# Bias network of a deformable attention: the last addition by transfers, the third layer on four pairs of keys at a time

## Chip, core and metric

One NeuronCore of a Trainium2 chip runs the whole program in one launch. The metric is the device time in microseconds (us), float32 throughout. Engines are named as the profile names them: PE (TensorE, matrix products), PEld (its weight loads), DVE (VectorE), ACT (ScalarE), POOL (GpSimd) and SP (SyncE, which here only issues transfers).

## What is computed

The program is a chain of four blocks on a tensor of 2 x 512 x 32 x 32. The change lies in the first block, an attention with 8 heads whose 64 keys per (image, head) are sampled at learned positions. Every score gets a bias from a small network on the distance of query and key, evaluated for each of 8 x 2 x 1024 x 64 pairs:

```
pos  = grid_q[:, :, None, :] - grid_kv[:, None, :, :]
bias = sign(pos) * log1p(abs(pos))
bias = relu(bias @ cpb_w1 + cpb_b1)        # 2 -> 128
bias = relu(bias @ cpb_w2 + cpb_b2)        # 128 -> 128
bias = (bias @ cpb_w3 + cpb_b3)            # 128 -> 1
sim  = einsum('bhid,bhjd->bhij', qh, kh) + bias
attn = softmax(sim, axis=-1)
out  = einsum('bhij,bhjd->bhid', attn, vh)
x    = x + out_w @ out + out_b             # then a two-layer perceptron with gelu
```

Blocks 2 to 4 (another attention, a non-local block, a gated block) are not touched.

## The kernel before

**Stages.** A prologue normalises the input, projects queries (`query`), transposes the input (`flip_x`) and computes the first keys' positions (`Chain`). The main stage, a loop at line 910 over 256 pairs `p` of keys, evaluates the bias network and, between its pieces, everything else of the attention. Then come the projection `po` (L1014), the perceptron (L1079) and the other blocks.

**A key** here is one key of two heads, that is 2 x 1024 pairs; 8 groups `g` (4 pairs of heads, 2 images) of 64 keys make 512. The step number `n` in the text counts keys.

**First layer.** `first(n)` (L374, DVE) adds a row and a column feature and clips at zero, 128 hidden units by 1024 queries, once for each head, from a table `tab`. Tables come from DRAM (`tab_load`, L152, SP) for `TK` = 16 keys at a time and are scaled on ACT (`tab_scale`, L164). There are four buffers `h1`, so DVE runs at most two keys ahead.

**Second layer.** `second(p, o)` (L610, PE) multiplies by a quarter `o` of the 128 outputs, 32 columns at a time, so that four products, one for each 512 queries, lie side by side on the 128 partitions of `ph` (two buffers). ACT clips them and adds the bias into `r{o}` (L619). The quarters are arranged so that the third layer's weights could be taken into the second layer's: what is left of a weight is its sign. `combine` (L625, DVE) adds quarter 1 to 0 and quarter 3 to 2 with the relative sign `rel`. `join(p)` (L628, POOL) is a transfer that adds `r2` to `r0` in memory. In `r0` there are then 32 sums per query, on 32 partitions for each of four blocks of queries, for two keys `i`.

**Third layer.** `third(g, u)` (L651, PE) sums these with a column of signs `cw3` into `psims`, four keys a time, four products of 32 columns side by side. The scores' own product (`scores`, L636) is accumulated into the same bank.

**Attention.** `attend` takes a finished group: `evict` (ACT), `flip` (PE), `top`, `sub`, `total`, `norm` (DVE) and `exp` (ACT), `back` (PE), `keep_` (ACT). `prepare` makes the next group's keys and values, and `chain` the positions of later groups; its 36 taps (L221, DVE) run beside the network.

**Order.** Every instruction of this stage is pinned to the order in which the program issues it on its engine. `at(n, when, fn)` puts `fn` behind the second layer's product of step `n` (`when` 0 or 1: half a step), and the loop at line 910 runs it:

```
for p in range(NK // 2):
    for o in range(4):
        n = 2 * p + o // 2
        second(p, o)
        if o == 1 and p:
            combine(p - 1, 2)
            join(p - 1)
        elif o == 3:
            combine(p, 0)
        elif n + 2 < NK and o % 2 == 0:
            first(n + 2)
        run(n, o % 2)
```

A queue of transfers (SP's, POOL's) also works in this order: an issue that waits holds up what is behind it.

**Weights.** In the prologue `order` sorts the four quarters of each of 32 rows by the sign of the third layer's weight, so that the signs of 0 and 1, and of 2 and 3, are mostly equal for a row, with some 30 small operations on POOL.

Of the kernel before, what the change touches and what calls it, by code (L numbers as in the profile page):

```python
# [16 lines left out]
P = 128  # L17
# [4 lines left out]
TK = 16  # L22
# [14 lines left out]
    ("L0_conv_cpb_w1", 2), ("L0_conv_cpb_b1", 1), ("L0_conv_cpb_b2", 4), ("L0_conv_cpb_w3", 4),  # L37
# [18 lines left out]
_CONSTS = [("ident", P), ("grid", 2 * J), ("gridf", J), ("npx", 1), ("npy", 8), ("sel3", 2)]  # L56
_CAT, _n = {}, 0
# [3 lines left out]
NCONST = _n  # L61


@with_exitstack
def conv_seq(
# [5 lines left out]
    consts: bass.AP,  # L71
    qkv_w: bass.AP,
# [53 lines left out]
    with ExitStack() as ctx_l0:  # L126
# [21 lines left out]
        def tab_load(ch, j0=0):  # L148

            g, c0 = divmod(ch * TK, J)  # L150
            tab = tabp.tile([P, TK, 2, 2, 32], F32, name="tab")
            nc.sync.dma_start(  # L152
                tab[:, j0:].rearrange("p i h a q -> p (i h a q)"),
                fd[g, c0 + j0 : c0 + TK, :]
                .rearrange("j f -> (j f)")
                .unsqueeze(0)
                .to_broadcast([P, (TK - j0) * P]),
            )
            return tab
# [13 lines left out]
        cpbw = l0.tile([P, 2 * P], F32, name="cpbw")  # L173
# [18 lines left out]
        class Chain:  # L192
# [126 lines left out]
            def put(self, i, b):  # L319

                nc.sync.dma_start(
                    fd[(self.k0 + i) * B + b].rearrange("(i m) f -> m i f", m=4),
                    self.lg[b * J : (b + 1) * J, i * P : (i + 1) * P],
                )
# [7 lines left out]
        cw3 = l0.tile([P, 39], F32, name="cw3")  # L332
        rel = l0.tile([P, 2], F32, name="rel")

        def order(to, of, w3, pool):

            n = w3.shape[2]
            gp = nc.gpsimd
            m = pool(9 * n).rearrange("p (i n) -> p i n", n=n)
            g, same, swap, other, keep_ = (m[:, 0:4], m[:, 4], m[:, 5], m[:, 6], m[:, 7])  # L340
            tmp, nswap = m[:, 8], m[:, 0]
            pin(nc.vector.tensor_scalar(g, w3, 0.0, None, ALU.is_ge))
            for d, k in ((same, 2), (swap, 1)):
                gp.tensor_tensor(d, g[:, 0], g[:, k], ALU.subtract)
                gp.tensor_tensor(d, d, d, ALU.mult)
            gp.tensor_tensor(tmp, swap, same, ALU.mult)
            gp.tensor_tensor(swap, same, tmp, ALU.subtract)
            gp.tensor_scalar(same, same, -1.0, 1.0, ALU.mult, ALU.add)
            gp.tensor_tensor(keep_, swap, same, ALU.add)
            gp.tensor_scalar(other, keep_, -1.0, 1.0, ALU.mult, ALU.add)  # L350
            gp.tensor_scalar(nswap, swap, -1.0, 1.0, ALU.mult, ALU.add)

            def mix(i, *parts):
                t = pool(of.shape[2])
                for j, (k, mask) in enumerate(parts):
                    d = to[:, i] if j == 0 else t
                    gp.tensor_tensor(d, of[:, k], mask.to_broadcast([P, of.shape[2]]) if n == 1 else mask, ALU.mult)
                    if j:
                        gp.tensor_tensor(to[:, i], to[:, i], t, ALU.add)

            mix(0, (0, keep_), (1, other))
            mix(1, (1, same), (2, swap), (0, other))
            mix(2, (2, nswap), (1, swap))
            gp.tensor_copy(to[:, 3], of[:, 3])
# [22 lines left out]
        with tc.tile_pool(name="a", bufs=1) as a, tc.tile_pool(name="aps", bufs=3, space=PSUM) as aps, tc.tile_pool(  # L387
# [9 lines left out]
            qw = a.tile([P, KC, P], F32, name="qw")  # L397
            nc.scalar.dma_start(qw, qkv_w[:, 0])
# [4 lines left out]
            for k in range(1, KC):  # L403
                nc.sync.dma_start(xn[k].rearrange("p (b n) -> p b n", b=B), x_dram[k])
                if k == 1:
                    nc.sync.dma_start(offw, off_w)
                    nc.sync.dma_start(cpbw, cpb_w)
            nc.sync.dma_start(kvw, qkv_w[:, 1:3])
# [55 lines left out]
            room, used = h1p.tile([P, 2, 32, 32], F32, name="h1").rearrange("p h y x -> p (h y x)"), [0]  # L464

            def part(n):
                used.append(used[-1] + n)
                return room[:, used[-2] : used[-1]]

            wb = part(8).rearrange("p (s i) -> p s i", s=4)  # L470
            w3 = v("L0_conv_cpb_w3").unsqueeze(2)
            pin(nc.vector.tensor_scalar(wb[:, :, 0:1], w3, 0.0, 2.0, ALU.is_ge, ALU.mult))
            pin(nc.vector.tensor_scalar(wb[:, :, 0:1], wb[:, :, 0:1], -1.0, None, ALU.add))
            nc.gpsimd.tensor_tensor(wb[:, :, 1:2], w3, wb[:, :, 0:1], ALU.mult)
            nc.gpsimd.tensor_tensor(wb[:, :, 1:2], wb[:, :, 1:2], v("L0_conv_cpb_b2").unsqueeze(2), ALU.mult)
            order(sb3, wb, w3, part)
            for i in range(2):
                nc.gpsimd.tensor_tensor(rel[:, i : i + 1], sb3[:, 2 * i, 0:1], sb3[:, 2 * i + 1, 0:1], ALU.mult)
            nc.gpsimd.memset(cw3, 0.0)
            for t in range(4):  # L480
                ts_ = slice(32 * t, 32 * t + 32)
                nc.gpsimd.tensor_copy(cw3[ts_, 7 + 8 * t : 8 + 8 * t], sb3[ts_, 0, 0:1])
            w2r = part(P)
            w3r = cpbw[:, P : 2 * P]
            pin(nc.scalar.activation(w2r, w3r, AF.Abs))
            nc.gpsimd.tensor_tensor(w2r, w2r, cpbw[:, 0:P], ALU.mult)
            order(w2a, w2r.rearrange("p (s o) -> p s o", s=4), w3r.rearrange("p (s o) -> p s o", s=4), part)
# [32 lines left out]
            query(2, 0)  # L520
            ch.offsets()
# [13 lines left out]
            ch.feature()  # L535

            tab0 = tabs[0] = tabp.tile([P, TK, 2, 2, 32], F32, name="tab")
            for u0 in range(0, 8, 4):
                pfb = apk.tile([P, 4, 2, 2, 32], F32, name=f"pfb{u0}")
                for u in range(4):  # L540
                    key = 16 * u + u0 // 4
# [13 lines left out]
            for b in range(B):  # L555
                ch.put(0, b)
                if b == 0:
                    nc.sync.dma_start(
                        tab0[:, 8:].rearrange("p i h a q -> p (i h a q)"),
                        fd[0, 8:TK, :].rearrange("j f -> (j f)").unsqueeze(0).to_broadcast([P, 8 * P]),  # L560
                    )
            tabs[1] = tab_load(1)
            ch.spread(1)
            ch.coordinate(1)
            first(0)
            queried(2, 1, 2)
# [3 lines left out]
            flip_x(1, 3, act)  # L570
            queried(2, 3)
# [5 lines left out]
            for k in range(2, KC):  # L577
                for t in range(NT // 512):
                    flip_x(k, t, dve)
                    flipped(k, t)  # L580
                if k == 2:
                    first(1)

# [4 lines left out]
        with tc.tile_pool(name="hid", bufs=3) as hid, tc.tile_pool(name="sm", bufs=1) as sm, tc.tile_pool(name="hps", bufs=2, space=PSUM) as hps, tc.tile_pool(  # L588
# [40 lines left out]

            def scores(g):  # L630
# [15 lines left out]
            def third(g, u):  # L646
                kb, i = divmod(u, 8)
                p = (g * J + 4 * u) // 2
                for m in range(4):
# [3 lines left out]
                            lhsT=cw3[:, 7 - i : 39 - i],  # L653
                            rhs=rs[p + m // 2, 0][:, m % 2, :],
                            start=False,
                            stop=(i == 7),
# [3 lines left out]
                for i in range(2):  # L660
                    del rs[p + i, 0]

            def prepare(g):
# [53 lines left out]
                def keys():  # L717

                    for half in range(2):
                        for h in range(2):  # L720
                            hs = slice(h * DH, (h + 1) * DH)
                            to = kblk[hs, g % 2, :, half, :].rearrange("p k (m s i) -> p s k m i", m=4, s=4)
                            pin(
                                nc.scalar.activation(
                                    to[:, 2 * half + h],
                                    st["pk"][hs, 0, :].rearrange("p (m k i) -> p k m i", m=4, k=2),
                                    AF.Identity,
                                    scale=DH**-0.5,
                                )
                            )  # L730

                def values():
                    for h in range(2):
# [3 lines left out]
                                vblk[hs, g % 2, h, :].rearrange("p (k m i) -> p k m i", k=2, m=4),  # L737
                                st["pk"][hs, 1, :].rearrange("p (m k i) -> p k m i", m=4, k=2),
# [36 lines left out]
            def attend(g, n, step):  # L775
# [4 lines left out]
                def evict(kb):  # L780
                    if kb == 0:
                        st["simt"] = sm.tile([P, 2, 512], F32, name="simt")
# [16 lines left out]
                def top(kb):  # L799
                    if kb == 0:  # L800
                        st["mx"] = sm.tile([P, 2, 16], F32, name="mx")
                        st["e"] = sm.tile([P, 16, J], F32, name="e")
# [24 lines left out]

                def norm(i):
                    den, is_ = st["den"], slice(8 * i, 8 * i + 8)
                    if i == 0:  # L830
                        pin(nc.vector.reciprocal(den, den))
                    e = st["e"][:, is_]
                    pin(nc.vector.tensor_tensor(e, e, den[:, is_].unsqueeze(2).to_broadcast([P, 8, J]), ALU.mult))
# [12 lines left out]
                def keep_(s):  # L846
# [6 lines left out]
                    (10, 0, exp, 0), (11, 0, exp, 1), (12, 0, exp, 2), (13, 0, exp, 3),  # L853
                    (14, 1, total, 0), (16, 1, total, 1), (18, 1, norm, 0), (20, 1, norm, 1),
                    (22, 1, back, 0), (22, 1, back, 1), (23, 0, keep_, 0), (23, 1, keep_, 1),
# [10 lines left out]
            for i in range(4):  # L866
                ax, j = i % 2, 8 + 4 * (i // 2)
# [838 lines left out]
```

## Time and profile before

| what | value |
|---|---|
| median of three runs | 2807.63 us (2806.73 to 2810.03) |
| the profiled execution | 2807.81 us, of which the span is 2806.0 us |
| prologue, 0 to 47 us | PE busy 34.39 us |
| bias network, 47 to 2002 us | PE busy 1951.08, DVE 1867.33, ACT 1324.89, POOL 219.55 us of 1955 |
| `po`, 2002 to 2051 us | PE busy 48.14 us |
| rest, 2051 to 2806 us | PE busy 724.05 us |

In a group's row of the profile, `out<-in xcount | busy, mean ns | idle before, releaser`, the idle time is that of the engine just before these instructions. A float32 product is recorded as two MATMULs. A transfer's time to landing counts from its issue to its semaphore.

### The profile page before, as it was taken

The page shows a single profiled execution, that of the slowest core. Times are in us where ns is not written, and L with a number is a line of the kernel's source. Part 1 is how long each engine was busy: PE and PEld are TensorE (multiplying, and loading weights), DVE is VectorE, ACT ScalarE, POOL GpSimd, SP SyncE. Part 2 cuts the span into 40 slices and gives each one's busy share as a digit, 9 for nine tenths or more (in the row PEclk, how much of TensorE's full clock was granted, in tenths as well). Part 3 has the DMA queues.
Part 4 walks back from the last instruction along what each step waited for, and adds up shares of the span by engine and source line. Part 5 has one row for each costly group of instructions (what it writes and reads, how often), then busy time and mean ns, then how long its engine had stood idle before and what let it go on. Part 6 is the DMA issues. An engine that isn't in the chain of part 4 may idle for free.

```text
span 2806.0 us, 47481 instructions
## 1 busy us (share of the span) xinstructions
PE 2757.7 (98%) x20280; PEld 1002.8 (36%) x20280; DVE 2275.4 (81%) x2473; ACT 1514.6 (54%) x1790; POOL 233.9 (8%) x318
## 2 busy tenths in 40 slices
PE   8999999999999999999999999999999999999996
PEld 4333333333333323333332333333344444455543
DVE  6999999999999999999999999999754554523545
ACT  6676676767667666766666676666311101001244
POOL 2111111111111111111111111111000000000000
PEclk9999999999999999999999999999999999999998
DMA  3444444434344443434453345443300000000001
GB/s 128 83 88 84 91 92 85 89 79 88 83 92 92 84 85 83 91 84 85 97 121 84 84 85 117 97 88 73 79 29 23 15 23 23 37 39 0 1 1 60
DMA packets 58835, 200.57 MB, mean 71 GB/s; under 512 B 5600, under 2 KB 14944, under 8 KB 53888
## 3 DMA queue, kind: packets, MB, share of 16 engines
q0 software_dynamic: 36864, 134.23, 25.5%
q1 hardware_dynamic: 21328, 62.79, 5.8%
q8 instruction: 159, 2.61, 0.4%
q10 hardware_dynamic: 432, 0.52, 0.1%
q14 instruction: 52, 0.43, 0.0%
HBM read 58.84 MB, written 4.46 MB: 23 GB/s over the span
## 4 chain that ended last, share of the span: by engine, by line
PE 53%; issue 37%; POOL 5%; DVE 2%; ACT 2%; DMA 0%; POOLq 0%; ACTq 0%; DVEq 0%
PE ph L610 24%; POOL r L628 5%; PE A L1079 4%; PE C L1079 4%; PE D L1079 4%; PE pr L1326 2%; PE B L1079 2%; PE po L1014 2%; PE psim L651 2%; PE pg L1222 1%; PE pz L1428 1%; PE pa L1317 1%; PE pu L1256 1%; PE pscore L1399 1%; PE pr L1439 1%
## 5 line engine op out<-in xcount | busy, mean ns | idle before, releaser
L610 PE MATMUL ph<-h,w2a 128*32 128x512 f32 x16384 | 1794.4, 593 | 2.2 <-ACT r L619 1.3
L619 ACT ACTIVATE r<-ph,sb 128x1024 f32<-128x1024 f32 x1024 | 1142.7, 1116 | 635.7 <-PE ph L610 617.9
L374 DVE CUSTOM_DVE_ANT_1 h<-tab 128x1024 f32<-128x1024 f32 x1024 | 1208.1, 1224 | 36.0 <-PE ph L610 35.4
L610 PEld LDWEIGHTS ph<-h,w2a 128*32 128x32 f32 x16384 | 533.4, 109 | 1213.6 <-issue 858.0
L625 DVE SCALAR_TENSOR_TENSOR r<-r,rel,r 128x1024 f32<-128x1024 f32 x512 | 657.7, 1285 | 32.7 <-ACT r L619 32.1
L628 POOL DMA_DIRECT2D r<-r x256 | 220.4, 861 | 1764.8 <-DVE r L625 1673.8
L164 ACT ACTIVATE tab<-tab,vec 128x256 f32<-128x256 f32 x252 | 137.3, 545 | 0.0
L651 PE MATMUL psim<-r,cw 128*32 128x512 f32 x1024 | 135.7, 593 | 0.8 <-DMA r<-r 0.8
L1119 ACT COPY u<-A 128x512 f32<-128x512 f32 x16 | 9.4, 586 | 146.9 <-PE A L1079 146.9
L1098 ACT ACTIVATE h<-h,vec 128x512 f32<-128x512 f32 x32 | 23.1, 721 | 113.3 <-DVE h L1101 113.3
L1101 DVE TENSOR_TENSOR h<-C,u 128x512 f32<-128x512 f32 x32 | 22.1, 691 | 48.1 <-PE C L1079 47.8
L1079 PE MATMUL A<-xn,w 128*128 128x512 f32 x128 | 60.2, 593 | 0.8 <-DVE x L1021 0.8
L651 PEld LDWEIGHTS psim<-r,cw 128*32 128x32 f32 x1024 | 33.9, 110 | 74.7 <-issue 73.7
L1079 PE MATMUL C<-hT,w 128*128 128x512 f32 x128 | 60.3, 592 | 0.0
L1079 PE MATMUL A<-h,w 128*128 128x512 f32 x128 | 60.1, 592 | 0.0
L1014 PE MATMUL po<-q,vwo 128*128 128x512 f32 x128 | 55.8, 594 | 0.0
L1326 PE MATMUL pr<-x,A 128*128 128x512 f32 x128 | 55.1, 592 | 0.0
L221 DVE SCALAR_TENSOR_TENSOR acc<-q,vec,acc 128x128 f32<-128x128 f32 (+3 forms) x88 | 46.9, 533 | 0.8
L1139 DVE TENSOR_TENSOR x<-D,x 128x512 f32<-128x512 f32 x32 | 22.1, 691 | 25.9 <-PE D L1079 25.9
L1139 DVE TENSOR_TENSOR x<-C,x 128x512 f32<-128x512 f32 x32 | 22.1, 690 | 24.8 <-PE C L1079 24.8
L1267 POOL MEMSET M<- 128x512 f32 x2 | 1.0, 524 | 443.9 <-DVE ss L1203 443.9
L1222 PE MATMUL pg<-xt 128*128 128x512 f32 (+3 forms) x128 | 36.4, 439 | 0.8 <-ACT xt L1220 0.6
(287 smaller groups left out, 1730.8 us busy)
## 6 DMA issues: line engine op xcount, KB each, us to landing
r<-r POOLq DMA_DIRECT2D x256, 512.0 KB, 4.5
tab<-fd SPq DMA_DIRECT2D x31, 1024.0 KB, 5.8
lw<-in_l_w_dram SPq DMA_DIRECT2D x5, 1024.0 KB
x<-in_x_dram SPq DMA_DIRECT2D x4, 1024.0 KB, 6.7
w<-in_mlp_w_dram SPq DMA_DIRECT2D x8, 512.0 KB, 3.7
w<-in_mlp_w_dram SPq DMA_DIRECT2D x16, 256.0 KB, 3.1
out_dram<-r SPq DMA_DIRECT2D x8, 512.0 KB, 2.7
xn<-in_x_dram SPq DMA_DIRECT2D x3, 1024.0 KB
```

The lines of the kernel that those rows point to most:

```text
L164: return nc.scalar.activation(tf, tf if src is None else src[:, :, :, ax, :], AF.Identity, bias=0.0 if ax == 0 else v("L0_conv_cpb_b1"), s ...
L221: pin(nc.vector.scalar_tensor_tensor(dst, src, wt_, dst, ALU.mult, ALU.add))
L374: nc.vector._custom_dve(TENSOR_ADD_SAT, out=h1[:, h], in0=tab[:, j, h, 0, :].unsqueeze(1).to_broadcast([P, 32, 32]), in1=tab[:, j, h, 1, : ...
L610: nc.tensor.matmul(ph[t * 32 : (t + 1) * 32, i, :], lhsT=w2a[:, o], rhs=h1s[2 * p + i][:, h, half * 512 : (half + 1) * 512], start=True, s ...
L619: pin(nc.scalar.activation(r, ph, AF.Relu, bias=sb3[:, o, 1:2]))
L625: pin(nc.vector.scalar_tensor_tensor(r0, r1, rel[:, i : i + 1], r0, ALU.mult, ALU.add))
L628: nc.gpsimd.dma_start(rs[p, 0], rs.pop((p, 2)), accum_op=ALU.add)
L651: nc.tensor.matmul(psims[g, kb][m * 32 : (m + 1) * 32, :], lhsT=cw3[:, 7 - i : 39 - i], rhs=rs[p + m // 2, 0][:, m % 2, :], start=False, s ...
L1014: nc.tensor.matmul(po, lhsT=vwo[:, k * B + t // 2, o * P : (o + 1) * P], rhs=q[:, k, ts_], start=(k == 0), stop=(k == KC - 1),)
L1079: nc.tensor.matmul(banks[bank], lhsT=a[an][k], rhs=b_[bn_][k], start=(i < 4 and k == 0), stop=(k == n - 1), skip_group_check=True,)
L1222: nc.tensor.matmul(pgs[i], lhsT=xt[:, i * P : (i + 1) * P], rhs=xt[:, i * P :], start=(t == 0), stop=(t == 7),)
L1326: nc.tensor.matmul(pr, lhsT=A[b][:, k, o * P : (o + 1) * P], rhs=x[:, k, ns], start=(k == 0), stop=(k == KC - 1),)
```

## The change

**The outputs that are left are added further.** After `join`, `r0` holds for each block of queries 32 sums for key 0 and 32 for key 1. The change adds neighbouring rows too: for key 0 the sums on odd partitions to the even ones, for key 1 the even to the odd. `shift(p)` is two SP transfers that copy the rows in question into a new tile `xs` (six buffers), one row aside; `fold(p)` is two POOL transfers that add the other rows of `r0`. Then `xs` holds 16 sums of each of the two keys, interleaved, on the 32 partitions. So a product of the third layer covers two keys, and four pairs of keys go into one set of four products.

**Positions.** `shift(p)` stands at step 2p + 4, `fold(p)` at 2p + 5, `third(g, u)` at 64g + 8u + 14 (before: at 64g + 4u + 6). Scores move from 64g + 6 to 64g + 10, the attention of a group by three steps, and its back part by six more.

**Signs.** All eight outputs that are added (four quarters of an even and an odd row) must stand so that each addition joins equal signs where it can. `order` goes. Instead the places are found by counting: two products with 0/1 matrices (`below`, `same`, from a new input `order`) count the positive weights of each eight, DVE works out a place for each, a permutation matrix `perm` is made, and further products permute the second layer's weights, its bias and the signs.

**Others.** The softmax's `norm` moves from two DVE operations per group to 16 ACT activations; `simt` shares `e`'s memory. `TK` becomes 8. The key and value layouts follow the new order of keys; a group's `keys` takes eight ACT copies, before four. The chains' starts move by 10 and 3 steps.

```diff
-TK = 16
+TK = 8
...
+            w3 = v("L0_conv_cpb_w3")
+            od = a.tile([P, 9], F32, name="od")
...
+            pin(ve.tensor_scalar(pos, w3, 0.0, None, ALU.is_ge))
+            pin(ve.tensor_scalar(sg, pos, 2.0, -1.0, ALU.mult, ALU.add))
+            pin(ve.tensor_tensor(maj, w3, sg, ALU.mult))
+            pin(ve.tensor_tensor(bs, maj, v("L0_conv_cpb_b2"), ALU.mult))
+
+            def counted():
+                pin(ve.tensor_scalar(cpbw, cpbw, maj, None, ALU.mult))
+                pin(ve.tensor_copy(od[:, 7:9], pcnt))
...
+                pin(ve.scalar_tensor_tensor(perm, oc("place"), t1, oc("same"), ALU.is_equal, ALU.mult))
+
+            def placed():
+                pin(ve.tensor_copy(w2a.rearrange("p s o -> p (s o)"), pw2))
+                to = perm.rearrange("p (s o) -> p s o", s=4).unsqueeze(2).to_broadcast([P, 4, 4, 32])
+                pin(ve.tensor_copy(wide, to))
+
+            def spread_out():
+                pin(ve.tensor_copy(sb3, psb))
+                pin(ve.tensor_tensor(rel, sb3[:, 0:4:2, 0], sb3[:, 1:4:2, 0], ALU.mult))
+                pin(ve.tensor_scalar(cw3, oc("third"), sb3[:, 0, 0:1], None, ALU.mult))
...
             query(2, 0)
+            pcnt = apk.tile([P, 2], F32, name="pcnt", tag="pfb0")
+            for i, m in enumerate(("below", "same")):
+                pin(nc.tensor.matmul(pcnt[:, i : i + 1], lhsT=oc(m), rhs=pos, start=True, stop=True))
             ch.offsets()
...
             ch.feature()
+            counted()
...
+            pw2 = apk.tile([P, P], F32, name="pw2", tag="pfb0")
+            pin(nc.tensor.matmul(pw2, lhsT=cpbw, rhs=perm, start=True, stop=True))
             first(0)
+            placed()
             queried(2, 1, 2)
             flipped(1, 1)
             query(2, 3)
             flip_x(1, 2, act)
             flip_x(1, 3, act)
+            psb = apk.tile([P, 4, 2], F32, name="psb", tag="pfb4")
+            for o in range(4):
+                to = wide[:, o].rearrange("p t o -> p (t o)")
+                pin(nc.tensor.matmul(psb[:, o], lhsT=to, rhs=od[:, 1:3], start=True, stop=True))
+            spread_out()
             queried(2, 3)
             flipped(1, 2, 3)
             query(3, 0, 1, 2, 3)
...
+            def shift(p):
+
+                r = rs[p, 0]
+                xs = rs[p] = hid.tile([P, 512], F32, name="xs", bufs=6)
+                for i in range(2):
+                    nc.sync.dma_start(xs[i::2], r[1 - i :: 2, i, :])
+
+            def fold(p):
+                r = rs.pop((p, 0))
+                for i in range(2):
+                    nc.gpsimd.dma_start(rs[p][i::2], r[i::2, i, :], accum_op=ALU.add)
+
...
             def third(g, u):
-                kb, i = divmod(u, 8)
-                p = (g * J + 4 * u) // 2
+                kb, i = divmod(u, 4)
+                p = (g * J + 8 * u) // 2
                 for m in range(4):
                     pin(
                         nc.tensor.matmul(
                             psims[g, kb][m * 32 : (m + 1) * 32, :],
-                            lhsT=cw3[:, 7 - i : 39 - i],
-                            rhs=rs[p + m // 2, 0][:, m % 2, :],
+                            lhsT=cw3[:, 3 - i : 35 - i],
+                            rhs=rs.pop(p + m),
                             start=False,
-                            stop=(i == 7),
+                            stop=(i == 3),
                             skip_group_check=True,
                         )
                     )
...
                 def norm(i):
-                    den, is_ = st["den"], slice(8 * i, 8 * i + 8)
-                    if i == 0:
-                        pin(nc.vector.reciprocal(den, den))
-                    e = st["e"][:, is_]
-                    pin(nc.vector.tensor_tensor(e, e, den[:, is_].unsqueeze(2).to_broadcast([P, 8, J]), ALU.mult))
+                    e = st["e"][:, i]
+                    pin(nc.scalar.activation(e, e, AF.Identity, scale=st["den"][:, i : i + 1]))
...
-                    (14, 1, total, 0), (16, 1, total, 1), (18, 1, norm, 0), (20, 1, norm, 1),
-                    (22, 1, back, 0), (22, 1, back, 1), (23, 0, keep_, 0), (23, 1, keep_, 1),
+                    (14, 1, total, 0), (16, 1, total, 1), (17, 1, inverse),
                 ]
+                plan += [(19 + i // 2, i % 2, norm, i) for i in range(16)]
+                plan += [
+                    (29, 0, back, 0), (29, 0, back, 1), (29, 1, keep_, 0), (30, 1, keep_, 1),
                 ]
...
             for g in range(NG):
                 prepare(g)
-                at(J * g + 6, 0, scores, g)
-                for u in range(16):
-                    at(J * g + 4 * u + 6, 1, third, g, u)
+                at(J * g + 10, 0, scores, g)
+                for u in range(8):
+                    at(J * g + 8 * u + 14, 0, third, g, u)
                 if g < NG - 1:
-                    attend(g, J * (g + 1) + 4, True)
+                    attend(g, J * (g + 1) + 7, True)
+            for p in range(NK // 2):
+                at(2 * p + 4, 0, shift, p)
+                at(2 * p + 5, 0, fold, p)
...
-            chain(1, 2, 72, 68)
-            chain(2, 4, 203, 118)
+            chain(1, 2, 82, 78)
+            chain(2, 4, 206, 114)
```

## The prediction

> **What bounds the kernel now.** I read the page's slices first, then busy time by stage, the costliest groups, and the timeline of one steady stretch and of the stage's end.
>
> ```profile
> DVE  6999999999999999999999999999754554523545
> ACT  6676676767667666766666676666311101001244
> ```
>
> ```profile
> 47.00:2002.00 1955.00, 1951.08 (x17907) 608.65 (x17907) 1867.33 (x1731) 1324.89 (x1477) 219.55 (x255) 1.00 0.42 88
> ```
>
> The bias network runs from 47 to 2002 us, 1955 of the 2806 us. The columns after the length are PE, PEld, DVE, ACT and POOL busy, then clock, DMA share and GB/s. PE idles 4 us in it, DVE 88, ACT 630. So PE sets this stage and DVE stands close behind.
>
> ```profile
> L610 PE MATMUL ph<-h,w2a 128*32 128x512 f32 x16384 | 1794.4, 593 | 2.2 <-ACT r L619 1.3
> L619 ACT ACTIVATE r<-ph,sb 128x1024 f32<-128x1024 f32 x1024 | 1142.7, 1116 | 635.7 <-PE ph L610 617.9
> L374 DVE CUSTOM_DVE_ANT_1 h<-tab 128x1024 f32<-128x1024 f32 x1024 | 1208.1, 1224 | 36.0 <-PE ph L610 35.4
> ...
> L625 DVE SCALAR_TENSOR_TENSOR r<-r,rel,r 128x1024 f32<-128x1024 f32 x512 | 657.7, 1285 | 32.7 <-ACT r L619 32.1
> L628 POOL DMA_DIRECT2D r<-r x256 | 220.4, 861 | 1764.8 <-DVE r L625 1673.8
> ...
> L651 PE MATMUL psim<-r,cw 128*32 128x512 f32 x1024 | 135.7, 593 | 0.8 <-DMA r<-r 0.8
> ```
>
> Busy PE time overlaps, so I take pitches from the timeline. Weight loads come four at a time, 0.43 us apart: four 32-column products run side by side, and each product is two records.
>
> ```profile
> 999.21 2.35 DVE L374 CUSTOM_DVE_ANT_1 h<-tab 128x1024 f32<-128x1024 f32 x2
> ...
> 999.59 0.86 POOL L628 DMA_DIRECT2D r<-r  x1 [6.06 <-DVE r L625]
> 999.71 0.61 PE L651 MATMUL psim<-r,cw 128*32 128x512 f32 x4
> ...
> 1000.14 0.13 PEld L610 LDWEIGHTS ph<-h,w2a 128*32 128x32 f32 x4 [0.30 <-issue]
> ...
> 1000.57 0.13 PEld L610 LDWEIGHTS ph<-h,w2a 128*32 128x32 f32 x4 [0.30 <-issue]
> ...
> 1001.48 1.28 DVE L625 SCALAR_TENSOR_TENSOR r<-r,rel,r 128x1024 f32<-128x1024 f32 x1
> ```
>
> Per key (512 keys), PE: second layer 16384/4/512 = 8 groups x 0.43 = 3.44 us; third layer 1024/4/512 = 0.5 group = 0.215; the stage is 1955/512 = 3.82, so all else (scores, samples, transposes) is 0.16. DVE from differences of starts: two L374 take 1001.48 - 999.21 = 2.27 us, one L625 1.20 (1008.70 to 1009.90 later in that answer), together 3.47.
>
> **What the Trainium skill says.** "TensorEngine Tiling (Array Packing)", Key Properties: tiles load and multiply in parallel, and a change of tiling mode drains the array. The trace agrees on the first (four in 0.43 us); second and third layer are both 128*32, so no drain is added. "DMA: Bandwidth & Descriptors", Rules for kernel authors: accumulation goes from GpSimd, and two transfers to disjoint halves of the partitions share the same 16 engines; no run here shows the latter yet. "SBUF — State Buffer", Who interferes with whom: a GpSimd DMA's descriptors are held up by DVE only in its two-port modes. The trace agrees: L628 takes 859 ns in minimum and median under a DVE that is 95% busy.
>
> **The change, part by part.**
>
> *Third layer.* One set of four products now serves eight keys, not four: 256 groups become 128. 128 x 0.43 = **-55.0 us**. It lies on PE, the path that sets the end. Per key PE falls to 3.44 + 0.11 + 0.16 = 3.71 us. That the products fall by half follows from the loops, so "it does not do what it says" gets no chance.
>
> *DVE as the next bound.* DVE per key: 3.47, and attention. Its eight 128x512 operations at 0.68 to 0.69 per (image, group) lose the two norms (L833, 690 ns) to ACT; the other six and cross, less 0.085 of overlap each, and small ones come to 5.9 us per 64 keys = 0.09. That is 3.56 against PE's 3.71: hidden. But the taps (L221) add to it. Chain 2's 36 taps are 23.8 us by their rows (21 x 0.700, 12 x 0.641, 3 others), less overlap 20.7, over 114 keys = 0.18: 3.74. Chain 1's are some 12.7 us over 78 keys = 0.16: 3.72. There DVE is late next: 114 x 0.03 + 78 x 0.01 = 4 us, and as queues between two engines so close do not average out I take **+7** (0 to 20).
>
> *Shift and fold.* Per pair of keys two SP transfers (64 rows x 2 KB, 128 KB each) and two accumulating POOL transfers of the same size. No row of before has such a form, so bounds:
> - DMA engines: a join costs 25.5% x 2806 x 16 / 256 = 44.7 engine-us for 512 KB; the folds, half its bytes, 22.4 by bytes, 44.7 if a 2 KB packet costs as much as a 4 KB one. Shifts at q1's rate (62.79 MB in 5.8%) 10.9. Tables 5.4. Sum 83 to 106 of 16 x 7.42 = 119 per pair: 70 to 89%. It fits.
> - POOL: 0.86 for the join and at most 2 x 0.86 = 2.6 of 7.42 us.
> - Latency: PE passes key 2p+3 when join p is issued (999.59 against L651 at 999.71) and comes to the third layer that needs the last pair's fold at key 2p+8.5: 5.5 x 3.71 = 20.4 us. Needed: join 4.5 us to landing; shift 3.1 (the page's 256 KB loads); POOL first issues join p+1, 0.86; folds 0.86 + 4.5. Sum 13.8. Hidden, with 6.6 us to spare. The low end, a gain from the removed wait of the third layer for joins, is 1 us (L651 idle 0.8).
> - What queues behind the waits: on POOL, fold p waits for shift p, and join p+2 stands behind it, due some 7 us later. On SP shifts stand behind table loads, which wait for L374 to free a table; the load is placed one key after that L374 is issued and the next shift two keys on, so nothing is late. r0 (four buffers) is wanted again at key 2p+8.5, the same limit.
>
> I take 0, and the high end goes to the rival below.
>
> *Tables* of 8 keys, not 16: 63 loads of half the size, the same number of L164 scalings. One such load of 1 MB took 5.8 us; a half one has four keys, 15 us, before its scaling: 0.
>
> *Norm on ACT*: 16 activations of 128x64 per group. Price: the skill's "ScalarE: Activation LUTs", What ACT_TABLE_LOAD costs, gives 280 ns + 0.833 per element with a pointer operand, an estimate of 333 ns (for the trace's 128x128 it gives 387, L672 shows 390). ACT has 1.72 us per eviction of 1.12: 1.12 + 0.33 fits; with a scaling (0.545) it is 0.27 over and the next slot, without one, gives it back. 112 x 0.33 = 37 us in 630 idle: 0 (0 to 3).
>
> *Moved positions*: scores, eviction and back come some keys later; scores stand three keys, 11 us, after evictions of 0.68: 0. Four more key copies on ACT per group (0.22 each): 0.
>
> *Before the stage.* POOL's sorting goes; 14 small DVE operations (0.17 to 0.29 by the rows of that stretch) come. Eleven, 2.2 us, fall into DVE's gap from 30.3 to 34.3. But the pfb bank is now shared with the counts (+0.4), and the four tiny psb products stand before query(3) on PE and wait for `wide`, which DVE copies after first(0): 34.7 + 2.35 + 0.29 + 0.69 = 38.0, where query(3) began at 35.8. So query(3) begins some 3 us later, and the flips behind it: **+3.5** (0 to 5).
>
> *After the stage.*
>
> ```profile
> 2003.19 5.38 PE L1014 MATMUL po<-q,vwo 128*128 128x512 f32 x12
> ...
> 2004.72 0.86 POOL L628 DMA_DIRECT2D r<-r  x1 [6.86 <-DVE r L625]
> ...
> 2009.36 1.05 PE L651 MATMUL psim<-r,cw 128*32 128x512 f32 x4 [0.79 <-DMA r<-r]
> ```
>
> The last third layer now waits for join, shift and fold: at the bounds above 3.1 + 0.86 + 4.5 = 8.5 us more, and 16 norms (16 x 0.24 back to back) are 2.6 more than two L833: 11 us. Half of L1014 needs nothing of it (64 records, 27.5 us; 32 stood here), so cover is there if the order on PE uses it: **+3** (0 to 11).
>
> **Sum**: -55.0 + 7 + 3.5 + 3 = -41.5. The profiled execution takes 2807.8 (span 2806.0 and 1.8 around it), the median of the runs is 2807.6, so it holds for both: **2766**. Own range: 2807.8 - 55 - 1 = 2752 to -55 + 20 + 5 + 11 + 3 = 2792.
>
> **Rivals.**
> *The fold comes late (slower).* If the second shift waits for the first and the second fold for the first (their rows interleave in one tile), the chain is 13.8 + 3.1 + 4.5 = 21.4 us, past the 20.4 at which it decides; at 70 to 89% DMA load another half us is easy. Each us over is paid at 64 third layers. At 1.5 us over: 96 - 42 = +54, **2862**. For it: the form is untried here and DMA load nearly doubles. Against it: that sum takes a 128 KB transfer at the price of a 512 KB one. 0.13.
> *DVE takes the gain.* DVE's share of the stage would be 1867 - 10 of 1900, 98%. If each close passage costs both engines their buffers (two keys ahead) it loses 0.08 us per key: 40 us, **2806**. Against it: 80 to 200 us, where DVE is busy 118.15 of 120 us, PE is at 120.00 of 120. 0.07, a part of it below the bound.
> *The forecast*: 0.80.
>
> What this kernel's runs can tell from no change is about 0.2%, 5.6 us (they spread from 2806.7 to 2810.0). Chances: faster 0.80, within it 0.06, slower 0.14. Range 2752 to 2800: it takes in the forecast with its unknowns and the DVE case in part, and leaves the slow rival out.
>
> **What would show it.** L651 at 512 records; the stage near 1910 us; L374 waiting for PE less than 35 us, and PE waiting for L374 between keys 92 and 206; SP and POOL issues of xs at 512 each, landing in under 4.5 us; L651 waiting for DMA only at the end. PE idle before L651 in each eighth key, or ACT waiting for r0, would make the prediction wrong.

## The result and the profile after

The changed kernel takes **3254.55 us**, the median of four runs (3251.75 to 3259.28), against 2808.28 us of the kernel before beside it. The ratio is 1.1591, 95% interval 1.1571 to 1.1611: 446 us slower, where 42 us faster was forecast. The profiled execution took 3259.28 us, of which 3257.5 us is span.

From its first second-layer product to its last (L610 before, L614 after) the stage of the bias network takes 2388.7 us (51.6 to 2440.3) where it took 1954.1 us (47.2 to 2001.3). That is 434.6 of the 451.5 us by which the span has grown (the start gives 4.4 more, what follows the stage 12.5): 9.33 us per pair of keys against 7.63. The granted clock of this stage is 0.97 where it was 1.00, 3% beside the stage's 22%; the pinned kernel below has 1.00 again with the same transfers. From the page of the changed kernel, the busy tenths in slices of the span, the chain that ended last, the groups and the transfers:

```profile
PE   8978888888888888888888888888889999999996
DVE  6888888888888777777776877778765444543455
ACT  6555565556556655555565555555541211110144
...
DMA 44%; PE 38%; issue 6%; POOL 5%; ACT 4%; DVE 3%; POOLq 0%; SPq 0%; ACTq 0%; DVEq 0%
...
L614 PE MATMUL ph<-h,w2a 128*32 128x512 f32 x16384 | 1894.7, 612 | 376.6 <-ACT r L623 375.5
L623 ACT ACTIVATE r<-ph,sb 128x1024 f32<-128x1024 f32 x1024 | 1130.4, 1113 | 1065.1 <-DMA r<-r 596.0
...
L629 DVE SCALAR_TENSOR_TENSOR r<-r,rel,r 128x1024 f32<-128x1024 f32 x512 | 656.5, 1282 | 425.2 <-ACT r L623 423.6
L644 POOL DMA_DIRECT2D xs<-r x512 | 443.9, 1007 | 1731.4 <-DMA xs<-r 1563.2
L632 POOL DMA_DIRECT2D r<-r x256 | 379.7, 1483 | 63.6 <-DVE r L629 61.3
...
L667 PE MATMUL psim<-xs,cw 128*32 128x512 f32 x512 | 76.3, 640 | 6.4 <-DMA xs<-r 6.4
...
r<-r POOLq DMA_DIRECT2D x256, 512.0 KB, 5.3
xs<-r SPq DMA_DIRECT2D x512, 128.0 KB, 2.0
xs<-r POOLq DMA_DIRECT2D x512, 128.0 KB, 3.0
```

Read it from PE backwards. PE idles 377 us before L614 for ACT, where it idled 2.2 us. ACT idles 596 us before its eviction L623 for a DMA: the join still reads the `r2` that the eviction wants to write, and `r2` has two buffers. The trace shows that it is this buffer: in 228 of 254 pairs the eviction into `r2` starts 0.08 us after the landing of the join of two pairs before; in the kernel before, in none. DVE's combine waits for ACT too, so none of the three engines is the bound. The third layer (L667) has half as many products as before and hardly waits. The odd row is L644, the fold: POOL sits 1563 us before it, waiting for `xs<-r`, the shift. And L632, the join, no longer waits for the combine (1674 us before, 61 us now): it is always late. The timeline shows the order on POOL (the rows in between are left out):

```profile
1002.69 1.71 POOL L644 DMA_DIRECT2D xs<-r  x2 [8.46 <-DMA xs<-r]
...
1003.85 1.44 POOL L632 DMA_DIRECT2D r<-r  x1
...
1009.20 1.10 SPq L639 DMA_DIRECT2D xs<-r  x2
...
1011.71 1.71 POOL L644 DMA_DIRECT2D xs<-r  x2 [6.42 <-DMA xs<-r]
...
1012.78 1.53 POOL L632 DMA_DIRECT2D r<-r  x1
```

One lap: join at 1003.85, its landing releases the shift at 1009.20 (5.35), the shift's releases the folds at 1011.71 (2.51), and only behind these the next join is issued at 1012.78 (1.07). That is 8.93 us, with no work of PE, ACT or DVE in it, and no slack: over pairs 4 to 249 the median time from the join's landing to the shift's issue is 0.12 us, from the shift's landing to the fold's issue 0.55, and from the second fold's issue to the next join's 0.54. Over the stage the median lap is 9.1 us and the mean 9.37. PE needs 7.42 for a pair, by the prediction's sum.

So **fold p stands ahead of join p+1 on POOL**. In program order it stands behind it: the loop issues join p+1 at step 2p+4, and `at` puts fold p at 2p+5. The compiled order of POOL's queue in the changed kernel (`r_3084` is `r0` of pair p, `r_3117` its `r2`):

```
L632 r_3084<-r_3117 128x1024      # join p
L644 xs<-r_3084 64x512 x2         # fold p
L632 r_3148<-r_3181               # join p+1
L644 xs<-r_3148 x2                # fold p+1
```

The reason is in the code: `join`, `shift` and `fold` issue their transfers without `pin(...)`, which leaves their place on the queue to the compiler. The sentence in the part on the kernel before, that every instruction of this stage is pinned, is wrong for the transfers: these three, and the table loads, are not. The kernel before had an unpinned join too, but nothing else stood beside it on POOL in this stage.

### The profile page after: what moved, and what is told of

It is laid out like the page before. It is cut to its first block, busy times and chain, and to the rows that moved or that the text cites. A ratio compares the mean times of both kernels' runs of the same rounds, so it can differ in the third digit from the quotient of the medians.

```text
span 3257.5 us, 49921 instructions
## 1 busy us (share of the span) xinstructions
PE 2826.2 (87%) x19782; PEld 971.4 (30%) x19782; DVE 2303.2 (71%) x2473; ACT 1523.9 (47%) x1950; POOL 668.3 (21%) x776
## 4 chain that ended last, share of the span: by engine, by line
DMA 44%; PE 38%; issue 6%; POOL 5%; ACT 4%; DVE 3%; POOLq 0%; SPq 0%; ACTq 0%; DVEq 0%
DMA r<-r 33%; PE ph L614 13%; DMA xs<-r 11%; POOL xs L644 5%; PE A L1099 3%; PE D L1099 3%; PE C L1099 3%; ACT r L623 2%; PE pr L1346 2%; PE B L1099 2%; PE po L1034 1%; PE pg L1242 1%; DVE h L349 1%; PE pz L1448 1%; PE pa L1337 1%
## 5 line engine op out<-in xcount | busy, mean ns | idle before, releaser
L614 PE MATMUL ph<-h,w2a 128*32 128x512 f32 x16384 | 1894.7, 612 | 376.6 <-ACT r L623 375.5
L623 ACT ACTIVATE r<-ph,sb 128x1024 f32<-128x1024 f32 x1024 | 1130.4, 1113 | 1065.1 <-DMA r<-r 596.0
L614 PEld LDWEIGHTS ph<-h,w2a 128*32 128x32 f32 x16384 | 513.2, 112 | 1710.9 <-issue 871.3
L644 POOL DMA_DIRECT2D xs<-r x512 | 443.9, 1007 | 1731.4 <-DMA xs<-r 1563.2
L632 POOL DMA_DIRECT2D r<-r x256 | 379.7, 1483 | 63.6 <-DVE r L629 61.3
L667 PE MATMUL psim<-xs,cw 128*32 128x512 f32 x512 | 76.3, 640 | 6.4 <-DMA xs<-r 6.4
L850 ACT ACTIVATE e<-e,den 128x64 f32<-128x64 f32 x128 | 41.7, 337 | 2.6 <-DVE den L846 2.6
```

What stands on the lines that cost most here:

```text
L614: nc.tensor.matmul(ph[t * 32 : (t + 1) * 32, i, :], lhsT=w2a[:, o], rhs=h1s[2 * p + i][:, h, half * 512 : (half + 1) * 512], start=True, s ...
L623: pin(nc.scalar.activation(r, ph, AF.Relu, bias=sb3[:, o, 1:2]))
L632: nc.gpsimd.dma_start(rs[p, 0], rs.pop((p, 2)), accum_op=ALU.add)
L644: nc.gpsimd.dma_start(rs[p][i::2], r[i::2, i, :], accum_op=ALU.add)
L667: nc.tensor.matmul(psims[g, kb][m * 32 : (m + 1) * 32, :], lhsT=cw3[:, 3 - i : 35 - i], rhs=rs.pop(p + m), start=False, stop=(i == 3), ski ...
```

## The experiments

Theory A: the order on POOL closes the ring join, shift, fold, next join, and all else follows. Its rivals: the transfers as such cost the time, in whatever order (B); the other parts of the change do (C: norms on ACT, signs, tables); or it is the pinning and not the order that makes the difference (D). For what is lost in the right order: DVE is the next bound (E), or PE's own gaps are (F).

**Pinning the three transfers.**

```diff
-                nc.gpsimd.dma_start(rs[p, 0], rs.pop((p, 2)), accum_op=ALU.add)
+                pin(nc.gpsimd.dma_start(rs[p, 0], rs.pop((p, 2)), accum_op=ALU.add))
...
-                    nc.sync.dma_start(xs[i::2], r[1 - i :: 2, i, :])
+                    pin(nc.sync.dma_start(xs[i::2], r[1 - i :: 2, i, :]))
...
-                    nc.gpsimd.dma_start(rs[p][i::2], r[i::2, i, :], accum_op=ALU.add)
+                    pin(nc.gpsimd.dma_start(rs[p][i::2], r[i::2, i, :], accum_op=ALU.add))
```

> The changed kernel with join, shift and fold held to the order in which the program names them, so that POOL issues join p+1 before fold p; nothing else differs. Theory A (order: fold p stands straight behind join p, and join p+1 behind it, so join, shift and fold of one pair follow those of the pair before in a ring of 9.0 us): the ring is open, the time is that of the prediction, 2750 to 2790 us. Theory B (the transfers themselves are too slow: 16 engines 58% busy, a join's issue 1.48 us instead of 0.86 and its landing 5.3 us instead of 4.5): same transfers, so 3150 to 3255 us. Theory C (the other parts, norms on ACT, signs, tables): 3200 to 3255 us.

Measured: **2766.88 us** (2765.39 to 2767.68), ratio to the kernel before 0.9853 (0.9838 to 0.9867). The compiled orders of DVE and ACT are the same as in the changed kernel, PE's differs after the stage, where one third-layer product stands behind four of the projection, not ahead of them; SP's differs in two places. POOL's now reads join p, fold p-1, join p+1, fold p. Groups and transfers of this kernel's page:

```profile
L614 PE MATMUL ph<-h,w2a 128*32 128x512 f32 x16384 | 1790.7, 593 | 7.0 <-ACT r L623 6.9
...
L644 POOL DMA_DIRECT2D xs<-r x512 | 474.2, 1137 | 195.4 <-PE ph L614 110.8
L632 POOL DMA_DIRECT2D r<-r x256 | 222.0, 867 | 1110.2 <-DVE r L629 948.4
...
L850 ACT ACTIVATE e<-e,den 128x64 f32<-128x64 f32 x128 | 41.7, 337 | 2.9 <-DVE den L846 2.9
...
r<-r POOLq DMA_DIRECT2D x256, 512.0 KB, 4.7
xs<-r SPq DMA_DIRECT2D x512, 128.0 KB, 2.4
xs<-r POOLq DMA_DIRECT2D x512, 128.0 KB, 4.7
```

and its timeline:

```profile
811.76 0.86 POOL L632 DMA_DIRECT2D r<-r  x1 [5.05 <-DVE r L629]
...
816.86 1.10 SPq L639 DMA_DIRECT2D xs<-r  x2
...
820.88 0.86 POOL L632 DMA_DIRECT2D r<-r  x1 [6.51 <-DVE r L629]
...
821.41 2.06 POOL L644 DMA_DIRECT2D xs<-r  x2
```

Join p goes out at 811.76 and its shift at 816.86. Join p+1 goes out as soon as its combine is done, and fold p behind it. The lap shown, 9.12 us, is a long one, because the join waited for its combine; the median over the stage is 7.29 and the mean 7.45. The join again waits for DVE, not DVE for the join, and PE's idle time before L614 falls from 377 to 7 us. The transfers and all other parts of the change are still there, so B and C are out. A second measurement of this kernel:

> The pinned kernel once more, beside the tuned one on the same chip: 2765 to 2768 us.

Measured: 2767.67 us (2766.53 to 2768.37), 0.9856 (0.9843 to 0.987).

**The ring, with pins.** Does the order do it, or the pinning? Everything pinned, and fold p put one step earlier, which is ahead of join p+1:

```diff
-                at(2 * p + 5, 0, fold, p)
+                at(2 * p + 4, 0, fold, p)
```

> The pinned kernel with fold p named half a pair earlier (step 2p + 4, not 2p + 5), which puts it straight behind join p and ahead of join p+1 on POOL; the rest is as in the pinned kernel. Theory A (the order on POOL alone): the ring is closed again, some 9 us per pair, 3230 to 3260 us. Theory D (pinning helped by something else, such as SP's order or fewer waits between the engines): it stays at 2765 to 2800 us.

Measured: 3258.0 us, 1.1603 (1.1582 to 1.1624), median lap 9.16 us. The compiled orders of PE, ACT, DVE and SP are those of the pinned kernel; POOL's alone differs. The group of L614, from the page:

```profile
L614 PE MATMUL ph<-h,w2a 128*32 128x512 f32 x16384 | 1897.1, 612 | 374.9 <-ACT r L623 372.6
```

These are the changed kernel's 377 us again, from one position. Theory A is shown, D is out.

**The ring without its middle link.** In the changed kernel (unpinned) the shift copies from the tile of the pair before, so that it doesn't wait for join p; the sums it adds are then those of another pair.

```diff
-                r = rs[p, 0]
+                r = rs[max(p - 1, 0), 0]
...
-                r = rs.pop((p, 0))
+                r = rs[p, 0]
+                rs.pop((p - 2, 0), None)
```

> The changed kernel, not pinned, with shift p copying the rows of r0 of the pair before, which has long been joined; so the second key's neighbours are the wrong pair's. Same number and size of transfers, same order on POOL, but shift (some 2.5 us from join's landing to its own) is no longer a link of the ring. Theory A: the ring is join's 5.2 us to landing and 1.1 us to the next join's issue, 6.3 to 7 us per pair, less than PE's 7.4: 2765 to 2830 us. Theory B (the transfers' amount): 3150 to 3255 us.

Measured: 2916.97 us, 1.0389 (1.037 to 1.0407), 7.99 us per pair. This lies in neither range. The same number and size of transfers cost 338 us less once the shift's wait is out of the lap, which speaks against B once more. A is right in kind, but its size was missed: the ring of join and fold alone was expected to fit under PE's 7.4 us per pair and doesn't. From this kernel's timeline:

```profile
857.04 1.53 POOL L632 DMA_DIRECT2D r<-r  x1
...
863.12 1.71 POOL L645 DMA_DIRECT2D xs<-r  x2 [4.55 <-PE ph L614]
864.46 1.26 POOL L632 DMA_DIRECT2D r<-r  x1
...
871.73 1.71 POOL L645 DMA_DIRECT2D xs<-r  x2 [6.01 <-DMA r<-r]
872.80 1.53 POOL L632 DMA_DIRECT2D r<-r  x1
```

Laps of 7.42 and 8.34 us. One row names PE as what the fold waited for; yet in at least three pairs of four the fold goes out some 0.5 us after its own join's landing, long after its shift's. With 5.6 us from join to landing (median) and 1.07 from fold to next join, that is a lap of 7.2 us, not 6.3 to 7. The quarter of the laps that are shortest are within 7.14 us, the longest quarter are 8.6 and more, and a landing takes up to 10.6 us. That the ring passes each late landing on is a reading that no run here tests alone.

**What the transfers cost when nothing waits for them.** The changed kernel without shift and fold; the join is not pinned in it, but nothing else stands on POOL in the stage. The third layer reads the first key's half of `r0` of four pairs directly, so the second keys' sums are left out; `r0` gets seven buffers and the third layer comes three steps sooner.

```diff
-                r = hid.tile([P, 2, 512], F32, name=f"r{o}", bufs=(4, 1, 2, 1)[o])
+                r = hid.tile([P, 2, 512], F32, name=f"r{o}", bufs=(7, 1, 2, 1)[o])
...
-                            rhs=rs.pop(p + m),
+                            rhs=rs.pop((p + m, 0))[:, 0, :],
...
-                    at(J * g + 8 * u + 14, 0, third, g, u)
+                    at(J * g + 8 * u + 11, 0, third, g, u)
...
-            for p in range(NK // 2):
-                at(2 * p + 4, 0, shift, p)
-                at(2 * p + 5, 0, fold, p)
```

> The changed kernel without shift and fold: the third layer reads the first key's sums of r0 alone, so the second key of each pair and the addition of neighbours are left out; r0 has seven buffers and the third layer stands three keys earlier. It shows what all the rest costs with the halved third layer. Theories A and B: 2745 to 2770 us, PE bound. Theory C: above 3000 us.

Measured: 2758.67 us (2758.21 to 2759.67), 0.9825 (0.9809 to 0.9842). Its stage is 1901.6 us, the pinned kernel's 1907.1. So without the 512 shifts and 512 folds, and with the more room for `r0`, the stage is 5.5 us shorter and the whole 8. That is about what these transfers cost where no join waits behind them.

**How much room the third layer has.** The pinned kernel with the third layer two steps sooner:

```diff
-                    at(J * g + 8 * u + 14, 0, third, g, u)
+                    at(J * g + 8 * u + 12, 0, third, g, u)
```

> The pinned kernel with the third layer two keys, 7.4 us, earlier (64g + 8u + 12). In the pinned kernel the last fold lands 5.7 us before its third layer in the median. If a late fold is paid at each of 64 third layers, as the prediction's slower rival had it, PE stands 1.7 to 2.5 us each time: 2870 to 2930 us. If the chain of transfers moves up as PE waits, it costs less than 40 us: 2767 to 2807 us.

Measured: 2852.67 us, 1.0159 (1.0141 to 1.0178), 86 us over the pinned kernel or 1.34 us at each of 64 third layers. What PE waits for before L667 in this kernel, from the profile's view of that line:

```profile
  DMA xs<-r: 131.5, 88
```

This adds up two columns of the profile, 84.7 us before weight loads (PEld) and 46.9 before products (PE), and so is more than the 86 us that show in the time; the pinned kernel has 0.6 us. In the pinned kernel the last fold lands 5.6 us (median; the expectation has 5.7) before its third layer: two steps, 7.4 us, are more than that. The result lies between the two ranges that were expected, nearer to the one in which each late fold is paid.

**A version that beats both.** The pinned kernel with the four tiny `psb` products behind `query(3)`:

```diff
-            psb = apk.tile([P, 4, 2], F32, name="psb", tag="pfb4")
-            for o in range(4):
...
             queried(2, 3)
             flipped(1, 2, 3)
             query(3, 0, 1, 2, 3)
+            psb = apk.tile([P, 4, 2], F32, name="psb", tag="pfb4")
+            for o in range(4):
...
```

> The pinned kernel with the four small products psb behind query(3), the first of the tuned kernel's two edits alone. If the tuned kernel's gain is that of the start, 2763 to 2766 us; if it is that of the sums on ACT, 2767 to 2768 us.

Measured: 2764.79 us (2763.69 to 2765.15), 0.9845 (0.9831 to 0.9858).

The same, and the softmax's sums taken by ACT in 16 exponentials per group in place of DVE's reductions:

```diff
-                    (10, 1, exp, 0), (11, 1, exp, 1), (12, 1, exp, 2), (13, 1, exp, 3),
-                    (14, 1, total, 0), (16, 1, total, 1), (17, 1, inverse),
...
+                plan += [(10 + i // 2, i % 2, exp, i) for i in range(16)]
+                plan += [(18, 1, inverse)]
```

> The pinned kernel with two edits: the four small products psb stand behind query(3), and the softmax's sums are taken by ACT's accumulator in 16 activations per group, in place of four activations and two sums on DVE. Theory E (DVE, 97.5% busy in the stage, costs the 10 us by which the stage stays above what PE's products ask for): DVE loses 14 x 0.6 = 8 us there, and the stage starts 2 us earlier: 2757 to 2763 us. Theory F (PE's own gaps, not DVE): only the 2 us of the start, 2764 to 2766 us.

Measured: 2764.28 us (2762.26 to 2765.71), 0.9844 (0.9831 to 0.9857), 1.6% under the kernel before. It and the one above overlap, so the gain over the pinned kernel, some 3 us, comes with the first edit, that of the start. It is small: the one above reaches up to 2765.15 us, the pinned kernel's two measurements begin at 2765.39. Busy times of the stage, the pinned kernel's and this one's (PE, PEld, DVE, ACT, POOL, then clock, DMA share, GB/s):

```profile
49.00:1956.00 1907.00, 1897.13 (x17389) 591.47 (x17391) 1856.65 (x1717) 1351.30 (x1621) 656.69 (x763) 1.00 0.75 161
```

```profile
47.00:1955.00 1908.00, 1898.93 (x17395) 593.09 (x17395) 1850.16 (x1703) 1368.46 (x1818) 656.55 (x763) 1.00 0.75 161
```

DVE has 6.5 us less to do and the stage, first to last product, takes 1907.6 us as against 1907.1: it did not move. That is against E and for F, with one reserve: ACT has 17 us more to do here, and a gain that ACT took back is not excluded.

## Why the prediction was wrong

The step that failed is in "Shift and fold": "POOL first issues join p+1" and "fold p waits for shift p, and join p+2 stands behind it, due some 7 us later". That took the written order for the compiled one. With join p+1 in join p+2's place, the chain of join, shift and fold, 9.1 us in the median, is paid once per pair, against 7.42 us, and not once per third layer against 20.4 us of room. The term was put at 0; the runs show 1.88 us on each of 256 pairs (9.33 us of the changed kernel less 7.45 of the pinned one). The changed kernel and the pinned one are 488 us apart and differ in little but this order, and in the pinned kernel the move of one fold brings the whole loss back.

The sign that was named also missed: PE was to idle before the third layer, or ACT for `r0`. The wait came out one stage sooner, at ACT's eviction for `r2`, because a late join holds `r2`, which has two buffers. The slow rival had a late fold, but by another mechanism: it was priced at 64 third layers, while the loss fell on each of 256 pairs.

The rest of the sum can be read from the pinned kernel, which is the change in the order the prediction assumed. It gave 2766.88 us where 2766 was forecast. That agreement is in part luck, as the terms show; each is read from single executions, and the start differs by 2.3 us between two of the same kernel.

| term | forecast, us | pinned kernel, us | read from |
|---|---|---|---|
| stage: third layer and next bound | -55.0 + 7 = -48 | -47.0 | 1907.1 against 1954.1 |
| start of the stage | +3.5 | +1.9 (+4.3 in its second profile) | 49.1 and 51.5 against 47.2 |
| after the stage | +3 | +2.7 | span -42.4, less the two above |

- **Third layer, next bound.** The 8 us that the stage keeps back of 55 match the +7 in size. Their cause was to be DVE, and that is not borne out: lightening DVE changed nothing (with the reserve above), PE's idle time is for ACT (6.9 us), and 5.5 us of the 8 go when the transfers go. So the size was right by luck. How the transfers delay ACT, and what the other 2.5 us are, stays open.
- **Shift and fold.** In the right order, near nothing, as said. The sizes inside: a fold took 4.7 us to land behind a join (bound 4.5), a shift 2.4 (bound 3.1), DMA share 75% (70 to 89). Spare time was 5.6 us where 6.6 was worked out.
- **The rival's price.** Third layers that come before their folds do pay at 64 places: 1.34 us each when two steps are taken away, less than the 1.8 us that 7.4 less 5.6 gives.
- **Norms on ACT.** 337 ns where the Trainium skill's "ScalarE: Activation LUTs", What ACT_TABLE_LOAD costs, gave an estimate of 333. ACT had room for them.
- **Prologue.** In the pinned kernel the `psb` products begin at 37.27 us, and `query(3)` at 38.16 where it began at 35.83: 2.3 us of the "some 3". With them behind it, `query(3)` begins at 36.08.

## What to carry to other kernels

On a queue that works in order, look at each transfer that waits for a transfer: if the next independent one stands behind it, latencies add up to a ring. Where its lap is longer than what the engines need (here 9.1 us against 7.42), the lap and not any engine's busy time sets the loop. Read the order from the compiled queue or the trace, not from the program, and see that each issue is in fact bound to its place. An engine that waits for a DMA to free its output's buffer, while POOL waits long before an issue, is how this ring looked in the profile.

## What was unexpected of the hardware

- A fold of 64 rows (128 KB) costs POOL 0.84 us to issue, a join of 128 rows (512 KB) 0.86: the bytes hardly count. Two folds came to 1.71.
- Issues that follow one another overlap in POOL's rows. In the changed kernel the join's row starts 0.54 us (median) after that of the second fold and ends 0.89 us after its end. So the 1.53 us of a join behind two folds (1528 ns in the median) hold 0.64 us in which the fold's row was still open. From the end of its row the join lands in 3.75 us, where it took 3.69 in the kernel before. The join itself is thus hardly dearer: the longer issue and the 5.3 us to landing in place of 4.5, which the first expectation puts under theory B, are for the most part time behind the folds.
- A fold lands in 3.0 us when it is issued ahead of a join (changed kernel), in 4.7 us behind one (pinned kernel); from the end of its row 1.8 and 3.5.
